# An LSTM in a two-layer kernel: the sums of four gates in two PSUM tiles instead of four, two sets of them, and their seeds in wider products spread over three steps

## The chip, the cores and the metric

The kernel runs on one core of a Trainium2 chip. The metric is the device time in microseconds of one execution, as the median of repeated runs; all times below are microseconds unless they are marked otherwise. The engines are PE (TensorE, with its weight loads listed as PEld), DVE (VectorE), ACT (ScalarE), POOL (GpSimd) and SP (SyncE, which issues DMAs).

## What is computed

The reference is a model of two layers on x of shape (8, 512, 256). Each layer has four parts: a conditioning step, an attention, a second conditioning step that is a recurrence over the 512 time steps, and a feed-forward part. In the first layer the recurrence is an LSTM with 256 hidden values and a batch of 8, and it is the only part that the change touches:

```python
xW = jnp.einsum('ntd,dg->ntg', x, Wx) + b
def step(carry, xw_t):
    prev_h, prev_c = carry
    a = xw_t + prev_h @ Wh
    i = jax.nn.sigmoid(a[:, :Hdim])
    f = jax.nn.sigmoid(a[:, Hdim:2 * Hdim])
    o = jax.nn.sigmoid(a[:, 2 * Hdim:3 * Hdim])
    g = jnp.tanh(a[:, 3 * Hdim:])
    next_c = f * prev_c + i * g
    next_h = o * jnp.tanh(next_c)
    return ((next_h, next_c), next_h)
```

Each step needs the h of the step before, so the 512 steps form one chain. All data are float32.

## The kernel before

The kernel runs its stages one after the other: the first layer's attention with its edge sums, the LSTM (function `lstm`, line 592), the routed heads, the second layer's attention, and a second recurrence with a mixture of experts. Inside the LSTM the orders of PE, ACT and DVE are written out by hand (`manual_schedule`): each of these engines runs its instructions in the order in which the program's text issues them. The framework adds the semaphores that data and memory need; it doesn't reorder these three engines.

**One step.** The 1024 gate values of a batch row are spread over four groups of 32 partitions (j = 0 to 3), 64 columns for each gate in each group. Each of the four gates, in the order f, i, g, o, has a PSUM tile of its own of 128 x 64 (`pgf`, `pgi`, `pgg`, `pgo`, made on line 618's list `banks`, with the column at which the gate lies in a weight row of 256). Line 678 multiplies the last h (kept in `ring`) with `wh`: two halves of the contraction (k) times four groups (j) make 8 matmuls for a gate, which are 16 matmul and 16 weight-load instructions on PE. Four time steps share a tile: step `now` of a group of four uses rows 8 * now to 8 * now + 7 of each 32. Its products cover the rows before them too, which nobody reads any more. The products are added to what already lies in the tile.

Then DVE transposes each gate's tile in 32 x 32 blocks into `G` (line 684), in the order f, i, g, o, and after each, ACT takes the sigmoid or tanh (line 685). After g's transpose DVE multiplies the old cell with f (line 687), after o's it runs a scan that gives the new cell (line 692). ACT takes the tanh of the cell (`th`, line 694), DVE multiplies it with o and writes the new h into `ring` (line 695), and PE can start the next step.

**The seeds.** What the products are added to is x's projection for four time steps, `xw`, brought into the tile's rows by a product with a selection matrix `pick` (function `seed`, line 648; its matmuls are line 652). In the last step of each group of four, after the four gates' transposes, 16 matmuls (4 gates x 4 groups of partitions, 64 columns each) seed all four tiles for the next four steps. They are 32 matmul and 32 weight-load instructions.

**The pieces.** Work of other stages is cut into pieces that are issued behind the ring write of chosen steps: gating pieces (`rest`, lines 534 to 552: eight for each 16 steps, the first two with PE work, the others ACT and DVE work), pieces of adaptive weights (`extra`, lines 1079 to 1089: PE products, DVE adds, and SP's DMAs of the next `w`, `b` and of the result `wd`), and the projection of the next 16 time steps (`project`, lines 637 to 645: two POOL copies, then eight PE products of 256 columns, with four DVE adds). In a step without PE work in a piece, a product whose result nobody reads (`fill`, line 708) keeps PE occupied; a step that seeds counts as having PE work. Every eighth step also sums `ring` on DVE (`hpart`, line 711) and copies it on ACT (`hT`, line 712).

Of the kernel before, what the change touches and what calls it, by code (L numbers as in the profile page):

```python
# [10 lines left out]
F32 = mybir.dt.float32  # L11
# [8 lines left out]
P = 128  # L20
B = 8
S = 512
# [352 lines left out]
class Edges:  # L375


    G = 8
# [213 lines left out]
def lstm(K, hT, rest, weights, extra, pp):  # L592

    nc, inp = K.nc, K.inp
    ident, xT = K.ident, K.xT
    mm = nc.tensor.matmul
    TT = nc.vector.tensor_tensor
    XB = GT
    RB = 8
    with ExitStack() as es:
        wp = K.pool(es, "l_w")
        sp = K.pool(es, "l_s", 3)  # L610
        xp = K.pool(es, "l_xw", 2)
        psx = K.pool(es, "l_px", 1, PSUM)
        extra = extra(K.pool(es, "l_pa", 1, PSUM))
        psg = K.pool(es, "l_pg", 1, PSUM)
        wx, wh, bias = weights
        pick = wp.tile([P, XB, B], F32, name="pick")
        nc.vector.tensor_copy(pick, ident.rearrange("p (b t) -> p t b", b=B))
        rings = [wp.tile([P, 2, 1 + RB, B], F32, name=f"ring{i}") for i in range(2)]
        for t in rings:
            nc.vector.memset(t[:, :, 0], 0.0)  # L620
        banks = [(psg.tile([P, 64], F32, name=f"pg{n}"), at) for n, at in (("f", 64), ("i", 0), ("g", 128), ("o", 192))]
        NC = 2 * B
        lefts = [wp.tile([P, 2 * NC], F32, name=f"left{i}") for i in range(3)]
        rights = [wp.tile([P, 2 * NC], F32, name=f"right{i}") for i in range(3)]
        cells = [wp.tile([P, 2 * NC], F32, name=f"cell{i}") for i in range(3)]
        for t in (*lefts, *cells):
            nc.vector.memset(t, 0.0)

        def half(w, n):
            return w.rearrange("p (k b two) -> p two k b", k=2, two=2)[:, n]  # L630

        def project(t0, pools=(psx,)):

            xw = xp.tile([P, 1024], F32, name="xw", tag="xw")
            xc = xp.tile([P, 2, P], F32, name="xc", tag="xc")
            for k in range(2):
                nc.gpsimd.tensor_copy(xc[:, k].rearrange("p (b t) -> p b t", b=B), xT[:, k, :, t0 : t0 + XB])  # L637
            yield xw
            for n in range(4):
                c = slice(n * 256, n * 256 + 256)  # L640
                px = pools[n % len(pools)].tile([P, S], F32, name="px", tag=("px", "pv")[n % len(pools)])[:, 0:256]
                for k in range(2):
                    mm(px, xc[:, k], wx[:, k, c], start=(k == 0), stop=(k == 1))  # L643
                    if k == 1:
                        nc.vector.tensor_tensor(xw[:, c], px, bias[:, c], ALU.add)
                    yield True

        def seed(t, xw):
            for dst, at in banks:
                for j in range(4):  # L650
                    c = j * 256 + at
                    mm(dst[32 * j : 32 * j + 32], pick[:, t % XB : t % XB + 4].rearrange("p t b -> p (t b)"), xw[:, c : c + 64], start=True, stop=True)

        proj = project(0, (psx, pp))
        xw = next(proj)
        for _ in proj:
            pass
        proj = iter(())
        nxt = None
        seed(0, xw)  # L660
        for _ in range(3):
            next(rest)
        E = mybir.EngineType
        K.marks = []
        es.enter_context(K.tc.manual_schedule(engines={E.PE, E.Activation, E.DVE}))
        for t in range(S):
            ring, at, now = rings[t // RB % 2], t % RB, t % 4
            for dst, c in banks:
                for k in range(2):
                    if t == 0:  # L670
                        hp = K.h0T[:, k, :]
                    elif at == 0:
                        hp = rings[1 - t // RB % 2][:, k, RB]
                    else:
                        hp = ring[:, k, at - now : at + 1].rearrange("p t b -> p (t b)")
                    for j in range(4):
                        w = wh[:, k, j * 256 + c : j * 256 + c + 64]
                        mm(dst[32 * j : 32 * j + B * (now + 1)], hp, w, start=False, stop=(k == 1), skip_group_check=True)  # L678
            left, right, cell, was = lefts[t % 3], rights[t % 3], cells[t % 3], cells[(t - 1) % 3]
            sf = sp.tile([P, 2, B], F32, name="sf", tag="sf")  # L680
            so = sp.tile([P, 2, B], F32, name="so", tag="so", bufs=2)
            for n, (to, f) in enumerate(((sf, AF.Sigmoid), (half(right, 0), AF.Sigmoid), (half(left, 1), AF.Tanh), (so, AF.Sigmoid))):
                G = sp.tile([P, 2, 32], F32, name="G", tag=f"G{n}")
                nc.vector.transpose(G.rearrange("p k b -> p (k b)"), banks[n][0])  # L684
                nc.scalar.activation(to, G[:, :, B * now : B * now + B], f)  # L685
                if n == 2:
                    TT(half(right, 1), sf, half(was, 1), ALU.mult)
            if now == 3 and t + 1 < S:
                if (t + 1) % XB == 0:
                    xw = nxt  # L690
                seed(t + 1, xw)
            nc.vector.tensor_tensor_scan(cell, left, right, 0.0, ALU.mult, ALU.add)
            th = sp.tile([P, 2, B], F32, name="th", tag="th")
            nc.scalar.activation(th, half(cell, 1), AF.Tanh)  # L694
            K.marks.append(TT(ring[:, :, at + 1], so, th, ALU.mult))  # L695
            at = t % XB
            busy = now == 3
            if at in (8, 13, 15, 0, 1, 2, 3, 4):
                busy |= next(rest, None) is True
            if at in (1, 2, 7, 11):  # L700
                busy |= next(extra, None) is True
            if at == 4 and t - 4 + XB < S:
                proj = project(t - 4 + XB)
                nxt = next(proj)
            elif at in (5, 6, 8, 9, 10, 12, 13, 14):
                busy |= next(proj, None) is True
            if not busy:
                mm(psx.tile([P, S], F32, name="fill", tag="px")[:, 0:256], ident, wx[:, 0, 0:256], start=True, stop=True)
            if t % RB == RB - 1:
                done = ring[:, :, 1:].rearrange("p k t b -> p k b t")  # L710
                nc.vector.tensor_reduce(K.hpart[:, t // RB % 16], done, AX.X, ALU.add)
                nc.scalar.copy(hT[:, :, :, t - RB + 1 : t + 1], done)
            if t % 64 == 5 and t > 64 or t == S - 3:
                n = t // 64
                n -= t < S - 3
                part = K.hpart[:, n % 2 * 8 : n % 2 * 8 + 7 + (n < 7)]
                nc.vector.tensor_reduce(K.hpart[:, 16 + n], part.rearrange("p n k b -> p k b n"), AX.X, ALU.add)
        for _ in extra:
            pass
# [685 lines left out]
XB = 16  # L1405
# [712 lines left out]
```

## Time and profile before

| what | us |
|---|---|
| median of 11 runs | 3889.5 (3885.09 to 3893.92) |
| the profiled execution, its device time | 3888.33 |
| its span, first to last instruction | 3886.6 |
| LSTM: start of the first ring write (L695) | 452.50 |
| LSTM: start of the last ring write | 1613.13 |
| the window 449 to 1614: PE busy, DVE busy, ACT busy | 939.68, 816.00, 611.89 |
| granted TensorE clock in that window, share of full speed | 1.00 |
| PE matmul and weight-load instructions in that window | 37845 and 37843 |

A row of the timeline gives the start from the span's begin, the duration, the engine, the line of the kernel, the operation, output and inputs, and how many instructions were merged (x16); in square brackets, how long the engine had been idle before and who released it. "issue" as releaser means that the engine waited for nothing that the profile shows. PE's matmuls overlap each other, so the durations of merged rows of two gates overlap too. A row of waits gives the time in total, the number of waits, and the longest.

### The profile page before, as it was taken

The numbers are of one execution on the slowest core, as the hardware profiler recorded it, in microseconds if no ns is written. First come the engines' busy times: TensorE is split into PE (matmuls) and PEld (weight loads), VectorE is DVE, ScalarE is ACT, GpSimd is POOL, SyncE is SP. The second block draws the span as 40 slices with busy tenths as digits, with TensorE's granted clock in tenths as the row PEclk, the third lists the DMA queues.
The fourth block names the chain that finished last, engine by engine and source line by source line (L and its number), as shares of the span: only waits on it lengthen the run. The fifth ranks groups of instructions, "written<-read, shape, count | busy, mean of one in ns | idle before, by whom it ended". The sixth has DMA issues, their size and how long they took to land.

```text
span 3886.6 us, 146241 instructions
## 1 busy us (share of the span) xinstructions
PE 3460.2 (89%) x62442; PEld 2319.0 (60%) x62442; DVE 2374.0 (61%) x8871; ACT 1618.1 (42%) x5695; POOL 668.3 (17%) x1479
## 2 busy tenths in 40 slices
PE   8999888888888888799989999999999899999986
PEld 5533455555555655466556666666666666666665
DVE  4488667767777767567657667666767533243444
ACT  3111255555555555455534444444444322232334
POOL 1010000000000000000023223222323111234366
PEclk9999999999999999999999999999999999999999
DMA  3022000000000000200000000000000060122245
GB/s 111 29 82 71 30 21 21 17 22 16 5 5 4 5 4 16 77 18 26 3 2 1 1 1 2 1 2 2 1 7 1 5 207 18 59 70 84 84 126 163
DMA packets 102924, 137.91 MB, mean 35 GB/s; under 512 B 12336, under 2 KB 84048, under 8 KB 102144
## 3 DMA queue, kind: packets, MB, share of 16 engines
q1 hardware_dynamic: 88416, 89.03, 7.4%
q0 software_dynamic: 11040, 34.29, 2.7%
q8 instruction: 490, 8.03, 0.9%
q10 hardware_dynamic: 2816, 5.24, 0.4%
q14 instruction: 162, 1.33, 0.1%
HBM read 86.44 MB, written 43.25 MB: 33 GB/s over the span
## 4 chain that ended last, share of the span: by engine, by line
PE 66%; ACT 14%; DVE 12%; issue 5%; POOL 1%; DMA 1%; ACTq 0%; POOLq 0%; SPq 0%; DVEq 0%
PE pgf L678 5%; PE pe L1237 4%; PE pg L1505 4%; PE po L1295 3%; PE pt L1280 3%; DVE G L684 3%; PE pp L1197 3%; PE pg L1738 3%; PE U L489 3%; PE px L1316 3%; PE pk L468 3%; ACT th L694 3%; ACT so L685 2%; PE pg L1484 2%; ACT left L685 2%
## 5 line engine op out<-in xcount | busy, mean ns | idle before, releaser
L678 PE MATMUL pgf<-wh,ring 128*16 128x64 f32 x8176 | 215.9, 223 | 201.6 <-DVE ring L695 198.4
L1508 DVE STREAM_TRANSPOSE ring<-h 128x64 f32<-128x64 f32 x512 | 125.6, 245 | 397.1 <-ACT h L1507 377.9
L678 PEld LDWEIGHTS pgf<-wh,ring 128*16 128x16 f32 x8176 | 127.8, 99 | 393.6 <-DVE ring L695 392.6
L1257 ACT ACTIVATE sm<-sm,nm 128x388 f32<-128x388 f32 (+3 forms) x512 | 283.6, 555 | 182.1 <-DVE nm L1253 182.0
L685 ACT ACTIVATE sf<-G 128x16 f32<-128x16 f32 x512 | 110.5, 216 | 464.2 <-DVE G L684 464.2
L1507 ACT ACTIVATE h<-pg 128x64 f32<-128x64 f32 x512 | 114.8, 224 | 453.2 <-PE pg L1505 400.5
L1505 PE MATMUL pg<-down,ring 128*16 128x64 f32 x8176 | 240.7, 223 | 30.5 <-DVE ring L1508 23.8
L1282 ACT COPY eT<-pt 128x512 f32<-128x512 f32 (+1 forms) x192 | 105.6, 550 | 357.4 <-PE pt L1280 357.2
L1197 PE MATMUL pp<-hn,wqkv 128*128 128x512 f32 x512 | 243.2, 619 | 0.8 <-DVE hn L1182 0.8
L1280 PE MATMUL pt<-ident,sm 128*128 128x128 f32 x1280 | 192.6, 283 | 56.8 <-DVE sm L1263 42.5
L1280 PEld LDWEIGHTS pt<-ident,sm 128*128 128x128 f32 x1280 | 148.1, 143 | 138.9 <-issue 81.9
L1264 POOL COPY pme<-sm 128x4 f32<-128x4 f32 x512 | 119.8, 235 | 646.5 <-DVE sm L1263 642.6
L678 PE MATMUL pgo<-wh,ring 128*16 128x64 f32 x8176 | 216.8, 220 | 14.2 <-issue 14.1
L678 PE MATMUL pgg<-wh,ring 128*16 128x64 f32 x8176 | 213.3, 220 | 4.8 <-issue 4.7
L684 DVE STREAM_TRANSPOSE G<-pgf 128x64 f32<-128x64 f32 x512 | 127.7, 249 | 138.7 <-PE pgf L678 132.7
L637 POOL COPY xc<-xT 128x128 f32<-128x128 f32 x64 | 17.1, 296 | 1136.0 <-DVE xT L552 1100.9
L678 PE MATMUL pgi<-wh,ring 128*16 128x64 f32 x8176 | 210.0, 220 | 1.2 <-issue 1.2
L1253 DVE CUSTOM_DVE_ANT_0 sm<-pe,mask 128x260 f32<-128x260 f32 (+2 forms) x384 | 141.7, 425 | 88.2 <-PE pe L1237 87.7
L1738 PE MATMUL pg<-xT,w 128*128 128x128 f32 x992 | 167.3, 295 | 17.8 <-POOL w L1718 12.7
L1263 DVE TENSOR_SCALAR sm<-sm,rc 128x388 f32<-128x388 f32 (+3 forms) x512 | 176.1, 387 | 9.0
L695 DVE TENSOR_TENSOR ring<-so,th 128x16 f32<-128x16 f32 x512 | 90.0, 176 | 147.3 <-ACT th L694 147.3
L643 PE MATMUL px<-wx,xc 128*128 128x256 f32 x512 | 174.4, 425 | 5.1 <-POOL xc L637 5.0
(513 smaller groups left out, 8284.5 us busy)
## 6 DMA issues: line engine op xcount, KB each, us to landing
cb<-order POOLq DMA_DIRECT2D x32, 512.0 KB
x<-xs SPq DMA_DIRECT2D x124, 128.0 KB
ys<-y SPq DMA_DIRECT2D x124, 128.0 KB
xs<-zero SPq DMA_DIRECT2D x66, 128.0 KB
w<-in_ada_w_dram SPq DMA_DIRECT2D x16, 512.0 KB
w<-in_moh_w_dram SPq DMA_DIRECT2D x32, 195.0 KB
xres<-xp SPq DMA_DIRECT2D x32, 128.0 KB
xc<-xres SPq DMA_DIRECT2D x32, 128.0 KB
```

Of the source, the lines that this page charges most:

```text
L643: mm(px, xc[:, k], wx[:, k, c], start=(k == 0), stop=(k == 1))
L678: mm(dst[32 * j : 32 * j + B * (now + 1)], hp, w, start=False, stop=(k == 1), skip_group_check=True)
L684: nc.vector.transpose(G.rearrange("p k b -> p (k b)"), banks[n][0])
L685: nc.scalar.activation(to, G[:, :, B * now : B * now + B], f)
L1197: mm(pp, T.wqkv[:, k, 0 : 2048].rearrange("p (i g h n) -> p i g h n", i=2, g=4, h=2)[:, i, g, h], self.hn[b][:, k, :], start=(k == 0), sto ...
L1237: mm(pe[a][:, 0 : w - lo], q[r, h, at], k[r, h, lo:w], start=(h == 0), stop=(h == 1))
L1253: nc.vector.tensor_tensor_reduce(out=sm[a][:, lo:w], in0=pe[a][:, 0 : w - lo], in1=T.mask[:, S - n + lo : 4 + S], scale=-1.0 / 8.0, scalar ...
L1257: nc.scalar.activation(sm[a][:, 0:w], sm[a][:, 0:w], AF.Exp, bias=nm[:, a : a + 1], scale=-1.0, accum_out=su[:, a : a + 1])
L1263: nc.vector.tensor_scalar(sm[a][:, 0:w], sm[a][:, 0:w], rc[:, a : a + 1], None, ALU.mult)
L1280: nc.tensor.transpose(pt[:, at, :], sm[i * m + a][:, 4 + j * P : 4 + (j + 1) * P], K.ident)
L1505: mm(pg[32 * j : 32 * j + B * (now + 1)], hp, M.wh[:, k, 64 * j : 64 * j + 64], start=False, stop=(k == 1), skip_group_check=True)
L1738: mm(pg, W[m][:, k * D + g * P : k * D + (g + 1) * P], X[m][:, k, :], start=(k == 0), stop=(k == 1))
```

## The change

The four tiles `pgf`, `pgi`, `pgg`, `pgo` are replaced by two tiles of 128 x 2 x 64, `pgig` (i in its first half, g in its second) and `pgfo` (f, then o), and there are two sets of these two tiles. A group of four time steps uses one set and the next group uses the other. A tile takes one PSUM bank, so the number of banks is four as before. The gates are still summed in the order f, i, g, o and transposed in the same order, each from its half.

A seed now brings in both gates of a tile with one product of 2 x 64 columns, for one group of partitions j: `seed(t, j, xw)` makes two matmuls of 128 columns. The seeds of the next group of four go into the other set, j = 0 and 1 in the first step of a group, j = 2 in the second and j = 3 in the third; the fourth has none. Eight matmuls replace sixteen. The projection that is being read (`xw = nxt`) is exchanged at step 12 of sixteen instead of step 15.

Of the pieces, the gating piece of step 8 of sixteen moves to step 14, and the projection's eight pieces, formerly in steps 5, 6, 8, 9, 10, 12, 13 and 14, are now in steps 5 to 12. A step that seeds no longer counts as one with PE work, so that each step without PE work in a piece gets a fill.

```diff
@@ -618,7 +618,8 @@
         rings = [wp.tile([P, 2, 1 + RB, B], F32, name=f"ring{i}") for i in range(2)]
         for t in rings:
             nc.vector.memset(t[:, :, 0], 0.0)
-        banks = [(psg.tile([P, 64], F32, name=f"pg{n}"), at) for n, at in (("f", 64), ("i", 0), ("g", 128), ("o", 192))]
+        banks = [[psg.tile([P, 2, 64], F32, name=f"pg{n}{i}") for n in ("ig", "fo")] for i in range(2)]
+        gates = [(1, 0, 64), (0, 0, 0), (0, 1, 128), (1, 1, 192)]
         NC = 2 * B
         lefts = [wp.tile([P, 2 * NC], F32, name=f"left{i}") for i in range(3)]
         rights = [wp.tile([P, 2 * NC], F32, name=f"right{i}") for i in range(3)]
@@ -645,11 +646,10 @@
                         nc.vector.tensor_tensor(xw[:, c], px, bias[:, c], ALU.add)
                     yield True
 
-        def seed(t, xw):
-            for dst, at in banks:
-                for j in range(4):
-                    c = j * 256 + at
-                    mm(dst[32 * j : 32 * j + 32], pick[:, t % XB : t % XB + 4].rearrange("p t b -> p (t b)"), xw[:, c : c + 64], start=True, stop=True)
+        def seed(t, j, xw):
+            x = xw[:, j * 256 : j * 256 + 256].rearrange("p (a g n) -> p g a n", a=2, g=2)
+            for g, dst in enumerate(banks[t // 4 % 2]):
+                mm(dst[32 * j : 32 * j + 32], pick[:, t % XB : t % XB + 4].rearrange("p t b -> p (t b)"), x[:, g], start=True, stop=True)
 
         proj = project(0, (psx, pp))
         xw = next(proj)
@@ -657,7 +657,8 @@
             pass
         proj = iter(())
         nxt = None
-        seed(0, xw)
+        for j in range(4):
+            seed(0, j, xw)
         for _ in range(3):
             next(rest)
         E = mybir.EngineType
@@ -665,7 +666,8 @@
         es.enter_context(K.tc.manual_schedule(engines={E.PE, E.Activation, E.DVE}))
         for t in range(S):
             ring, at, now = rings[t // RB % 2], t % RB, t % 4
-            for dst, c in banks:
+            for bank, a, c in gates:
+                dst = banks[t // 4 % 2][bank][:, a]
                 for k in range(2):
                     if t == 0:
                         hp = K.h0T[:, k, :]
@@ -681,28 +683,29 @@
             so = sp.tile([P, 2, B], F32, name="so", tag="so", bufs=2)
             for n, (to, f) in enumerate(((sf, AF.Sigmoid), (half(right, 0), AF.Sigmoid), (half(left, 1), AF.Tanh), (so, AF.Sigmoid))):
                 G = sp.tile([P, 2, 32], F32, name="G", tag=f"G{n}")
-                nc.vector.transpose(G.rearrange("p k b -> p (k b)"), banks[n][0])
+                nc.vector.transpose(G.rearrange("p k b -> p (k b)"), banks[t // 4 % 2][gates[n][0]][:, gates[n][1]])
                 nc.scalar.activation(to, G[:, :, B * now : B * now + B], f)
                 if n == 2:
                     TT(half(right, 1), sf, half(was, 1), ALU.mult)
-            if now == 3 and t + 1 < S:
-                if (t + 1) % XB == 0:
+            if now < 3 and t - now + 4 < S:
+                if t % XB == XB - 4:
                     xw = nxt
-                seed(t + 1, xw)
+                for j in ((0, 1), (2,), (3,))[now]:
+                    seed(t - now + 4, j, xw)
             nc.vector.tensor_tensor_scan(cell, left, right, 0.0, ALU.mult, ALU.add)
             th = sp.tile([P, 2, B], F32, name="th", tag="th")
             nc.scalar.activation(th, half(cell, 1), AF.Tanh)
             K.marks.append(TT(ring[:, :, at + 1], so, th, ALU.mult))
             at = t % XB
-            busy = now == 3
-            if at in (8, 13, 15, 0, 1, 2, 3, 4):
+            busy = False
+            if at in (13, 14, 15, 0, 1, 2, 3, 4):
                 busy |= next(rest, None) is True
             if at in (1, 2, 7, 11):
                 busy |= next(extra, None) is True
             if at == 4 and t - 4 + XB < S:
                 proj = project(t - 4 + XB)
                 nxt = next(proj)
-            elif at in (5, 6, 8, 9, 10, 12, 13, 14):
+            elif 4 < at < 13:
                 busy |= next(proj, None) is True
             if not busy:
                 mm(psx.tile([P, S], F32, name="fill", tag="px")[:, 0:256], ident, wx[:, 0, 0:256], start=True, stop=True)
```

## The prediction

> **What bounds the kernel now.** I read the page first, for the span and the costliest groups; then the timeline of a few recurrence steps, for the order inside one; then the starts of all 512 ring writes (L695), for how even the steps are; then PE's waits; and last one place of another stage that behaves as the new code will. The program has one long serial stage, the LSTM: the first ring write starts at 452.50 us, the last at 1613.13, so 1160.6 us hold 511 steps, 30% of the span. Inside it one step after the other looks like this:
>
> ```profile
> 1505.23 0.18 DVE L695 TENSOR_TENSOR ring<-so,th 128x16 f32<-128x16 f32 x1 [0.28 <-ACT th L694]
> ...
> 1505.46 0.42 PE L678 MATMUL pgf<-wh,ring 128*16 128x64 f32 x16 [0.49 <-DVE ring L695]
> ...
> 1505.92 0.41 PE L678 MATMUL pgg<-wh,ring 128*16 128x64 f32 x16
> 1505.94 0.25 DVE L684 STREAM_TRANSPOSE G<-pgf 128x64 f32<-128x64 f32 x1 [0.20 <-PE pgf L678]
> ...
> 1506.14 0.41 PE L678 MATMUL pgo<-wh,ring 128*16 128x64 f32 x16
> ...
> 1506.39 0.25 DVE L684 STREAM_TRANSPOSE G<-pgg 128x64 f32<-128x64 f32 x1
> ...
> 1506.67 0.22 ACT L685 ACTIVATE left<-G 128x16 f32<-128x16 f32 x1
> ...
> 1506.92 0.23 DVE L692 TENSOR_TENSOR_SCAN cell<-left,right 128x32 f32<-128x32 f32 x1
> ...
> 1507.18 0.22 ACT L694 ACTIVATE th<-cell 128x16 f32<-128x16 f32 x1
> ...
> 1507.43 0.18 DVE L695 TENSOR_TENSOR ring<-so,th 128x16 f32<-128x16 f32 x1 [0.28 <-ACT th L694]
> ```
>
> Columns are start, duration, engine, line, output and inputs. See the overlap: f's products end at 1505.88 (1505.46 + 0.42), and f's transpose starts 0.06 later, while PE still sums g and has o ahead of it. PE delivers a gate every 0.22 us and DVE turns each as it comes. So the period is a chain: 0.87 from PE's start to g's last product (1506.33), 0.06 to g's transpose, 0.28 to its tanh, 0.25 to the scan, 0.26 to th, 0.25 to the ring write, and 0.23 from there to PE's next start (1505.23 to 1505.46): 2.20. o is not in this chain. Its sums end at 1506.55 and its sigmoid at 1507.18, just as th begins. Of 511 steps, 446 take 2.19 to 2.24; I take 2.21. The rest of the 1160.6, 31 us above 511 x 2.21, sits in some sixty long steps, mostly the first of a group of four, and PE's waits show what they are:
>
> ```profile
> PE pgf L678 <- DVE ring L695: 198.4, 442, 1.6
> PE pgo L678 <- issue: 14.1, 22, 2.1
> PE pgg L678 <- issue: 4.7, 10, 0.8
> ```
>
> In these (us, times, longest) PE waits for nothing but its own instructions; all such waits of the stage add up to 21.9 us. The instruction queue moves 296 packets, 4.85 MB, during the stage.
>
> **The seeds today.** Every fourth step PE runs 64 more instructions (32 products, 32 weight loads; L652) after o's sums, 0.88 us in all, up to 1502.84 in the group that starts at 1501.96. The next step's PE start is 1503.26, 0.23 after its ring write, as in every other step. So the seeds cost nothing on the chain; they only lengthen the burst before the steps that stall for instructions.
>
> **The change, part by part.**
>
> (1) *f and o in one bank, i and g in another.* All four gates' sums are issued first, f, i, g, o, and then the transposes f, i, g, o (DVE keeps that order). If a read of one half of a bank has to wait for every earlier write to that bank, f's transpose waits for o's last product, the last of the step, and i's for g's. Is that so? L684 never shows it, as each gate has a bank to itself. The nearest row is another stage's tile po (L923, L925): sixteen products fill its first half, sixteen the second, and only then ACT reads the first half.
>
> ```profile
> 1935.29 2.71 PE L923 MATMUL po<-eT,v 128*64 128x128 f32 x32
> ...
> 1938.05 0.81 ACT L925 ACTIVATE oT<-po,bg,gh 128x128 f32<-128x128 f32 x2 [2.02 <-PE po L923]
> ```
>
> ACT sat idle 2.02 us. Fourteen of the first sixteen products had started by 1936.6, at 0.39 to 0.48 each, so the first half was whole by about 1937.2; ACT began at 1938.05, 0.05 after the last of the thirty-two. The read waited for the half that it doesn't touch. I take the same for f.
>
> The rule that speaks against the change is on the Trainium skill's page "PSUM — Partial Sum Buffer", in the section on bank collisions: two engines must not touch one bank in the same 32 partitions at once, even at different columns, so they have to be ordered by bank and not by address. By this rule f's transpose waits, and the stage gets longer as summed below; by the row that f's transpose starts 0.06 after f's own products, taken over unchanged, the period would stay 2.21. No run here shows a collision.
>
> Price: f's transpose moves from 0.48 after PE's start to o's end, 1.09 (1506.55 - 1505.46), plus 0.04 to 0.06 (0.06 for f at 1505.94; 0.04 for o in a step where PE stalled, 535.68 to 535.72). I take 1.14. What is late next: everything behind it on DVE's queue, i, g, the product L687, o, the scan; ACT's four functions wait for them, PE for the ring. But with all sums ready the transposes no longer wait for one another's sums. Steps that follow a hpart reduction (L711) show this in part, since f's transpose starts late there:
>
> ```profile
> 1503.84 0.24 DVE L684 STREAM_TRANSPOSE G<-pgf 128x64 f32<-128x64 f32 x1
> 1504.00 0.21 DVE L684 STREAM_TRANSPOSE G<-pgi 128x64 f32<-128x64 f32 x1
> ...
> 1504.19 0.25 DVE L684 STREAM_TRANSPOSE G<-pgg 128x64 f32<-128x64 f32 x1
> ...
> 1505.23 0.18 DVE L695 TENSOR_TENSOR ring<-so,th 128x16 f32<-128x16 f32 x1 [0.28 <-ACT th L694]
> ```
>
> From f's transpose to the ring write: 1.39 here, 1.49 in the normal step. g's still waited for its sum (0.93 after PE's start at 1503.26); at the 0.16 of f to i it would come 0.03 earlier, so 1.36 is the lower end and 1.40 (the slowest of such steps) the upper. I take 1.37, nearer the undisturbed case. New period: 1.14 + 1.37 + 0.23 = 2.74, with ends 1.13 + 1.36 + 0.23 = 2.72 and 1.16 + 1.40 + 0.23 = 2.79. Against 2.21: 0.53 a step, 512 x 0.53 = **+271 us** (261 to 297).
>
> (2) *Seeds of two gates in one product, over three steps.* 16 products for 32, each twice as wide (128 columns). The gate sums give the price: 16 instructions over four column groups in 0.22, so each group does four in 0.22, 55 ns for 64 columns, 110 for 128 as an estimate. One j is four instructions, 0.44; the first step's two j take 0.44 side by side or 0.88 in turn. Nothing is read back for four steps, since the other set of banks is filled: no wait on DVE. Cover: PE's end at 1.09, plus 0.88, plus a fill or a px piece of 0.70 is 2.67, inside 2.74; cost nothing. Had the period stayed 2.21, the same sum would be late by 0.02 to 0.46 in every fourth step (3 to 59 us). That is what the cover is worth.
>
> (3) *Pieces placed anew, and fills in each fourth step.* The gating pieces move from step 8 to 14 of sixteen, the projection pieces to 5 to 12. Their DVE work (0.42 to 0.49) and ACT work (0.40 to 0.61) lie between the ring write and f's transpose, a gap that grows from 0.72 to 1.37 us: nothing. SP's DMAs (w, b, wd in the extra pieces) and POOL's two copies keep their steps. The projection for a block now ends at step 12 of sixteen; j = 3 reads its last quarter in step 14. No wait there.
>
> (4) *The instruction waits.* PE issues 148 instructions a step now ((37845 + 37843) / 512), 65 per us. The change takes off about 8 a step and stretches the step: 140 in 2.74 us is 51 per us, and the burst of each fourth step is spread. The 31 us can lose anything from nothing to all; no row shows this rate, so I take the middle, **-16**.
>
> Sum on the profiled execution (3888.33 us, span 3886.6; median of the runs 3889.5, so nothing to correct): 3888 + 271 - 16 = 4143, rounded to **4145 us**.
>
> **Rivals.**
>
> *Halves are independent (6%).* f's transpose starts 0.06 after its own sums as now. Speaks for it: nothing but today's L684 rows, where banks are separate; against: po. The chain stays 2.21, the instruction waits lose about 16 to 20 us, and if the two j run side by side the seeds add 3: about **3873 us**, faster. It decides at f's transpose: under 0.6 us after PE's start, this one holds; at 1.1 mine does.
>
> *The order is the other way round (4%)*: g's products wait for i's transpose in the same bank. i's transpose ends 0.96 after PE's start (1506.17 + 0.25 - 1505.46); g then needs 0.42 as f does after a pause, and ends near 1.43 in place of 0.87. That is 0.56 a step, 287 us, less 16: **4159 us**, by another wait. Against it: in po nothing was read before the last write, and the sums are issued first. It decides at g's products: a pause of 0.5 before them on PE.
>
> *The wait comes and PE slows too (3%).* PE would be busy about 1.9 of 2.74 us. The stage's granted clock is 1.00; 36 us after it, between pauses of PE of 2.5 to 4.9 us, it is 0.81. At 0.81 the sums take 1.35 for 1.09: another 131 us, **4276**. Against it: gaps here stay below 1.3 us, as every step keeps a fill or a piece (2.74 - 1.09 - 0.43 for the shortest), and one of 2.10 us (L678, issue) changed no duration after it.
>
> **How the numbers follow.** My case has 87%. Its ends: 3888 + 261 - 31 = 4118 and 3888 + 297 = 4185, and 10 us more if the first seeds and a fill overrun in some steps; the range is 4115 to 4195, takes in the reversed order, and leaves out the other rivals (9%) and little else. Under 0.2% (8 us, about what the runs can tell from no change) is 1%, faster 5%, slower 94%.
>
> **What would show it.** In the profile after: ring writes 2.7 to 2.8 apart; f's transpose 1.1 after PE's start and waiting for the tile that holds f and o, the other three close behind at 0.16 to 0.19; the LSTM stage near 1405 us; the seeds on PE behind o's sums, waited for by nobody; PE's issue waits below 22. Everything after the stage should only be shifted. I am wrong if f's transpose still overlaps o's products.

## The result, and the profile after

The changed kernel takes 4112.7 us (median of 8 runs, 4107.65 to 4115.37), the kernel before on the same chip 3889.5 (31 runs). The ratio is 1.0572, with a 95% interval of 1.0563 to 1.0581: slower by 223 us. The forecast was 4145 with a range of 4115 to 4195, so its sign and mechanism hold and the median lies 2.3 us below the low end. What failed are two sizes in its sum; the section on the prediction names them.

The profiled execution took 4120.28 (span 4118.5), 7.6 more than the median and inside the range. I divide its span as the prediction divided that of before, by the ring writes (now L698):

| | before | after | difference |
|---|---|---|---|
| up to the first ring write | 452.50 | 456.19 | +3.7 |
| LSTM: 511 times the median step (2.21, 2.71) | 1129.3 | 1384.8 | +255.5 |
| LSTM: what is above that | 31.3 | 2.1 | -29.2 |
| behind the last ring write | 2273.5 | 2275.4 | +1.9 |
| sum: the span | 3886.6 | 4118.5 | +231.9 |

The median steps are rounded to 0.01 us here and below, which can move up to 2.6 us between the two LSTM rows.

One step in the timeline of after, to be held against the ten rows shown of before (weight loads left out):

```profile
1503.77 0.18 DVE L698 TENSOR_TENSOR ring<-so,th 128x16 f32<-128x16 f32 x1 [0.28 <-ACT th L697]
...
1504.00 0.43 PE L680 MATMUL pgfo<-wh,ring 128*32 128x64 f32 x16 [0.55 <-DVE ring L698]
...
1504.25 0.63 PE L680 MATMUL pgig<-wh,ring 128*32 128x64 f32 x32
...
1504.70 0.41 PE L680 MATMUL pgfo<-wh,ring 128*32 128x64 f32 x16
...
1505.17 0.25 DVE L686 STREAM_TRANSPOSE G<-pgfo 128x64 f32<-128x64 f32 x1 [1.22 <-PE pgfo L680]
1505.34 0.34 DVE L686 STREAM_TRANSPOSE G<-pgig 128x64 f32<-128x64 f32 x2
...
1505.80 0.24 DVE L686 STREAM_TRANSPOSE G<-pgfo 128x64 f32<-128x64 f32 x1
1505.98 0.22 DVE L695 TENSOR_TENSOR_SCAN cell<-left,right 128x32 f32<-128x32 f32 x1
...
1506.24 0.22 ACT L697 ACTIVATE th<-cell 128x16 f32<-128x16 f32 x1
1506.49 0.18 DVE L698 TENSOR_TENSOR ring<-so,th 128x16 f32<-128x16 f32 x1 [0.28 <-ACT th L697]
```

f's sums end at 1504.43. Its transpose starts at 1505.17, 0.06 after o's (1504.70 + 0.41): 1.17 after PE's start, where before it was 0.48. DVE has sat idle for 1.22, and the bracket names `pgfo`. i and g follow in 0.34 together. PE's sums themselves have not changed: 1.11 from the first to the last, as before (1.09). What has changed is that nothing is read while they run.

PE's waits in the stage (us, times, longest) show the other term:

```profile
PE pgfo L680 <- DVE ring L698: 346.5, 511, 1.3
...
PE pgfo L680 <- issue: 0.3, 1, 0.3
```

Before, 21.9 us of issue waits stood here, in 42 waits; one of 0.3 us is left. PE now waits for the ring write in every step.

### The profile page after: what moved, and what is told of

Its sections match the earlier page's. It is cut to its first block, busy times and chain, and to the rows that moved or that the text cites. A ratio compares the mean times of both kernels' runs of the same rounds, so it can differ in the third digit from the quotient of the medians.

```text
span 4118.5 us, 142417 instructions
## 1 busy us (share of the span) xinstructions
PE 3565.3 (87%) x60530; PEld 2393.1 (58%) x60530; DVE 2314.3 (56%) x8871; ACT 1483.8 (36%) x5695; POOL 661.3 (16%) x1479
## 4 chain that ended last, share of the span: by engine, by line
PE 68%; DVE 19%; ACT 6%; issue 4%; POOL 1%; DMA 1%; ACTq 0%; POOLq 0%; SPq 0%; DVEq 0%
PE pgfo L680 9%; DVE G L686 8%; PE pgig L680 6%; PE pe L1240 4%; PE pg L1508 4%; PE po L1298 3%; PE pt L1283 3%; PE pp L1200 3%; PE U L489 3%; PE pk L468 3%; PE px L1319 3%; PE pg L1741 3%; ACT so L687 3%; DVE ring L698 2%; PE pg L1487 2%
## 5 line engine op out<-in xcount | busy, mean ns | idle before, releaser
L680 PE MATMUL pgfo<-wh,ring 128*16 128x64 f32 x16352 | 423.1, 221 | 346.8 <-DVE ring L698 346.5
L680 PEld LDWEIGHTS pgfo<-wh,ring 128*16 128x16 f32 x16352 | 274.4, 99 | 549.3 <-DVE ring L698 548.6
L686 DVE STREAM_TRANSPOSE G<-pgfo 128x64 f32<-128x64 f32 x1024 | 252.3, 246 | 473.8 <-PE pgfo L680 473.8
L680 PE MATMUL pgig<-wh,ring 128*16 128x64 f32 x16352 | 321.9, 219 | 0.0
L680 PEld LDWEIGHTS pgig<-wh,ring 128*16 128x16 f32 x16352 | 261.0, 100 | 0.0
L1240 PE MATMUL pe<-kt,qt 32*128 32x132 f32 (+3 forms) x2048 | 178.9, 464 | 0.0
L1508 PEld LDWEIGHTS pg<-down,ring 128*16 128x16 f32 x8176 | 152.7, 99 | 41.9 <-DVE ring L1511 32.4
```

Of the source, the lines that this page charges most:

```text
L686: nc.vector.transpose(G.rearrange("p k b -> p (k b)"), banks[t // 4 % 2][gates[n][0]][:, gates[n][1]])
L1240: mm(pe[a][:, 0 : w - lo], q[r, h, at], k[r, h, lo:w], start=(h == 0), stop=(h == 1))
L1508: mm(pg[32 * j : 32 * j + B * (now + 1)], hp, M.wh[:, k, 64 * j : 64 * j + 64], start=False, stop=(k == 1), skip_group_check=True)
```

## Experiments

The chips differ: the kernel before takes 3885.9 us on that of the first four runs, 3844.9 on that of `e5` to `e7`, 3891.3 on that of `e8` to `e11`, and 3845.7 on that of `e12`. So each kernel stands beside the kernel before on its own chip. The last three columns are of the profiled executions: "LSTM" is the time from the first to the last ring write, "step" the median of its 511 steps, "excess" what they take above 511 times that rounded median.

| kernel | us | before | ratio (95%) | LSTM | step | excess |
|---|---|---|---|---|---|---|
| `e1_pairs_alone` | 4130.2 | 3885.9 | 1.0629 (1.0611 to 1.0647) | 1402.5 | 2.71 | 17.7 |
| `e2_if_go` | 3973.4 | 3885.9 | 1.0224 (1.0207 to 1.0241) | 1246.8 | 2.43 | 5.0 |
| `e3_turn_early` | 3923.2 | 3885.9 | 1.0097 (1.0080 to 1.0114) | 1197.8 | 2.34 | 2.1 |
| `e4_tile_two_banks` | 4148.9 | 3885.9 | 1.0674 (1.0654 to 1.0694) | 1425.8 | 2.71 | 40.9 |
| `e5_gate_bank_two_sets` | 3891.4 | 3844.9 | 1.0125 (1.0110 to 1.0141) | 1207.4 | 2.28 | 42.3 |
| `e6_burst` | 4079.3 | 3844.9 | 1.0616 (1.0600 to 1.0632) | 1393.9 | 2.71 | 9.0 |
| `e7_pieces_alone` | 3853.6 | 3844.9 | 1.0024 (1.0015 to 1.0033) | 1173.3 | 2.21 | 44.0 |
| `e8_before_plus16` | 3964.7 | 3891.3 | 1.0183 (1.0167 to 1.0198) | 1241.0 | 2.22 | 106.6 |
| `e9_after_plus64` | 4267.9 | 3891.3 | 1.0960 (1.0943 to 1.0976) | 1539.2 | 2.92 | 47.1 |
| `e10_fg_wide` | 3881.4 | 3891.3 | 0.9970 (0.9958 to 0.9982) | 1154.9 | 2.25 | 5.1 |
| `e11_fg_narrow` | 3885.9 | 3891.3 | 0.9986 (0.9977 to 0.9995) | 1161.8 | 2.26 | 7.0 |
| `e12_fo_early` | 3823.4 | 3845.7 | 0.9939 (0.9926 to 0.9953) | 1138.5 | 2.22 | 4.0 |

### Where the wait comes from

**Other pairs.** My theory: a transpose waits for every product that was issued before it into its tile. Then the pairs decide, and f with i, g with o must be cheaper. Edit to after:

```diff
-        ... for n in ("ig", "fo")] for i in range(2)]
-        gates = [(1, 0, 64), (0, 0, 0), (0, 1, 128), (1, 1, 192)]
+        ... for n in ("if", "go")] for i in range(2)]
+        gates = [(0, 1, 64), (0, 0, 0), (1, 0, 128), (1, 1, 192)]
```

> The changed kernel, but f shares a bank with i and g with o. If a read waits for every earlier write to its bank, f's transpose starts behind i's sums (about 0.70 us after PE's start), and g's behind o's (about 1.15); from g's transpose to the ring write it is 1.04 in the kernel before, perhaps 0.04 less, and 0.23 to PE's next start: a step of 2.38 to 2.42 where the changed kernel has 2.71, and 3935 to 3975 us in all. If the cost lies in something else of the change (products on half a tile, the wide seeds, the pieces, the fills), nothing moves: 4113 us and 2.71.

Measured: step 2.43, and the kernel is 87.5 us above its before where after is 223.2 above. f's transpose now waits for i's products, and g's for o's, each starting 0.06 to 0.07 after the end of the pair's sums:

```profile
1506.95 0.64 PE L680 MATMUL pgif<-wh,ring 128*16 128x64 f32 x32 [0.27 <-DVE ring L698]
...
1507.40 0.63 PE L680 MATMUL pggo<-wh,ring 128*16 128x64 f32 x32
1507.65 0.38 DVE L686 STREAM_TRANSPOSE G<-pgif 128x64 f32<-128x64 f32 x2 [0.43 <-PE pgif L680]
...
1508.10 0.25 DVE L686 STREAM_TRANSPOSE G<-pggo 128x64 f32<-128x64 f32 x1
```

**Other order, same tiles.** The tiles stay; DVE's reads are issued between PE's sums. Edit to after, in the loop over gates:

```diff
+            for m, (bank, a, c) in enumerate(gates):
...
+                for n in ((0,), (), (1, 2), ())[m]:
+                    turn(n)
```

> The changed kernel with its pairs of gates, but f's transpose is issued right behind f's sums, and those of i and g behind g's sums, ahead of o's. If the wait comes from the order in which sums and transposes of one bank are issued, f's transpose is back at 0.48 us after PE's start, i's comes at 0.93 and g's at about 1.06: a step of 2.30 to 2.34, and 3905 to 3930 us in all. If a bank with two gates is read only when both halves are whole, whatever the order of issue, it stays at 4113 us and 2.71.

Measured: step 2.34. The timeline of this kernel, weight loads left out:

```profile
1504.11 0.42 PE L685 MATMUL pgfo<-wh,ring 128*16 128x64 f32 x16
1504.34 0.63 PE L685 MATMUL pgig<-wh,ring 128*16 128x64 f32 x32
1504.59 0.25 DVE L672 STREAM_TRANSPOSE G<-pgfo 128x64 f32<-128x64 f32 x1 [0.21 <-PE pgfo L685]
1504.88 0.22 ACT L695 ACTIVATE sf<-G 128x16 f32<-128x16 f32 x1 [1.03 <-DVE G L672]
1504.90 0.42 PE L685 MATMUL pgfo<-wh,ring 128*16 128x64 f32 x16
1505.04 0.38 DVE L672 STREAM_TRANSPOSE G<-pgig 128x64 f32<-128x64 f32 x2 [0.20 <-PE pgig L685]
```

f's transpose is back at 0.48 after PE's start and runs while PE sums into the other tile. o's sums, issued behind it into the same tile, start at 1504.90, after the read's end at 1504.84. So the wait goes both ways, and the order in which sums and reads of one tile are issued decides who waits. Of the 0.50 lost, 0.37 return without a change of tiles. The other 0.13 are i's: its transpose stands behind g's sums, at 0.93 after PE's start in place of 0.71.

**Bank or tile?** The prediction said bank. Here before's four gates each have a bank of their own again, but in two tiles of two banks:

```diff
-        banks = [(psg.tile([P, 64], F32, name=f"pg{n}"), at) for n, at in ...]
+        tiles = [psg.tile([P, 2, 512], F32, name=f"pg{n}") for n in ("ig", "fo")]
+        banks = [(tiles[1][:, 0, 0:64], 64), (tiles[0][:, 0, 0:64], 0),
+                 (tiles[0][:, 1, 0:64], 128), (tiles[1][:, 1, 0:64], 192)]
```

> The kernel before (its seeds, its pieces), with f and o in one tile and i and g in another, but each tile two banks long and each gate in a bank of its own. If the wait goes by banks, nothing changes: 3889 us, give or take 8, and a step of 2.21. If it goes by tiles, f's transpose waits for o as in the changed kernel, and the seeds wait for o's transpose as well: a step of 2.71 or more, 4150 to 4250 us.

The timeline, weight loads left out:

```profile
1504.38 0.42 PE L679 MATMUL pgfo<-wh,ring 128*16 128x64 f32 x16
1504.61 0.63 PE L679 MATMUL pgig<-wh,ring 128*16 128x64 f32 x32
1505.06 0.41 PE L679 MATMUL pgfo<-wh,ring 128*16 128x64 f32 x16
...
1505.53 0.25 DVE L685 STREAM_TRANSPOSE G<-pgfo 128x64 f32<-128x64 f32 x1 [1.00 <-PE pgfo L679]
1505.70 0.34 DVE L685 STREAM_TRANSPOSE G<-pgig 128x64 f32<-128x64 f32 x2
```

f's transpose starts at 1.15, after o's last product, though o lies in another bank: the step is 2.71 as in after. The semaphores of this program go by tile. That is the framework's ordering, seen from its effect; whether two tiles in one bank would be ordered as well was not tried. The Trainium skill, page "PSUM — Partial Sum Buffer", section "PSUM bank collisions raise a hardware error", asks for a guard by bank and 32 partitions, and by that rule this kernel could have kept 2.21. The measurement decides: in this program a bank of one's own doesn't help inside a shared tile, a tile of one's own does.

### What the second set and the spread seeds are worth

The pairs alone, with one set of tiles, wide seeds in one burst, and before's places of pieces and fills; and the same with two sets. Edit to after for the latter, `e6_burst`:

```diff
-            if now < 3 and t - now + 4 < S:
+            if now == 3 and t + 1 < S:
...
-                for j in ((0, 1), (2,), (3,))[now]:
-                    seed(t - now + 4, j, xw)
+                for j in range(4):
+                    seed(t + 1, j, xw)
...
-            busy = False
+            busy = now == 3
```

with the lists of steps for the pieces as in before. For the former, `e1_pairs_alone`, one line more:

```diff
-        banks = [[psg.tile(...) ... for n in ("ig", "fo")] for i in range(2)]
+        banks = [[psg.tile(...) ... for n in ("ig", "fo")]] * 2
```

> One part of the change alone: the two tiles for four gates, but one set of them, all seeds (wide ones) in the last step of four, the pieces and fills as before. A step of 2.71 as in the changed kernel; and since the seeds now have to wait for o's transpose (it ends about 2.04 us after PE's start) and need about 1 us, each fourth step ends 0.35 to 0.5 late, 45 to 64 us in all: 4150 to 4195 us. If the second set of tiles buys nothing, as the seeds were hidden in the kernel before, it is 4113 to 4125 us.

> The changed kernel with its pairs and two sets, but the eight wide seeds all in the last step of four, and the pieces and fills of the kernel before. A step of 2.71. If slack on PE is what ends the instruction waits, they stay near 2 us: 4110 to 4118 us. If the burst makes them, some come back: 4118 to 4140. As PE has no pause of 1 us behind o's sums here, none of the steps of 3.5 us and more that the kernel with one set shows.

Measured: 244 us above before with one set, 234 with two and a burst, 223 in after. In all three the median step is 2.71; the pairing is the whole loss, and the rest of the change gives some 20 us of it back. I had the seeds of one set 0.35 to 0.5 late. They are not: PE waits 80.6 us for the transposes, starts the seeds 1.74 after its own start, and ends them at 2.75, just as the next step may begin: that step's sums start 0.23 after the ring write, as in before.

Part of what `e1`, `e4` and `e6` have above the median is something else, a fall of the TensorE clock. The timeline of `e6_burst`, PE's rows and the ring writes:

```profile
504.74 0.41 PE L680 MATMUL pgfo<-wh,ring 128*8 128x64 f32 x16 [1.14 <-DVE ring L698]
...
505.41 0.40 PE L680 MATMUL pgfo<-wh,ring 128*8 128x64 f32 x14
...
506.56 0.27 PE L680 MATMUL pgfo<-wh,ring 128*8 128x64 f32 x2 [0.75 <-issue]
506.77 0.99 PE L711 MATMUL fill<-wx,ident 128*128 128x256 f32 x2
508.19 0.18 DVE L698 TENSOR_TENSOR ring<-so,th 128x16 f32<-128x16 f32 x1 [0.28 <-ACT th L697]
508.42 0.63 PE L680 MATMUL pgfo<-wh,ring 128*16 128x64 f32 x16 [0.67 <-DVE ring L698]
508.82 1.08 PE L680 MATMUL pgig<-wh,ring 128*16 128x64 f32 x32
...
511.71 0.18 DVE L698 TENSOR_TENSOR ring<-so,th 128x16 f32<-128x16 f32 x1 [0.28 <-ACT th L697]
```

The same stretch by windows (start and end, length, busy time of PE, PEld, DVE, ACT and POOL with their instructions, granted clock, DMA share, GB/s):

```profile
506.00:507.00 1.00, 0.43 (x3) 0.32 (x3) 0.12 (x1) 0.00 (x0) 0.00 (x0) 1.00 0.00 0
507.00:508.00 1.00, 0.76 (x2) 0.06 (x1) 0.89 (x6) 0.65 (x5) 0.00 (x0) 0.52 0.06 16
508.00:509.00 1.00, 0.58 (x24) 0.58 (x28) 0.58 (x3) 0.16 (x2) 0.27 (x2) 0.50 0.00 0
```

At 507 the clock falls to one half, all sums take 1.5 to 1.7 times as long, and the step is 3.52. PE had paused 1.14 ahead of the row at 504.74 and 0.75 ahead of that at 506.56, with 1.1 us of sums in between. `e4` shows the same in the first step of a group (clock 0.50 from 1500.55 to 1503.96). Of the steps that lie more than 0.75 above the median (34 in `e4`, 13 in `e1`, 7 in `e6`, none in after), the clock falls in 31, 8 and 4. All steps with a fall hold about 31 of the 41 us of `e4`, 8 of the 18 of `e1` and 3 of the 9 of `e6`, where I had expected none; more than half of the rest are waits for instructions. The seeding step of these three kernels has no fill. The Trainium skill, page "TensorE: Matmul & The Clock Gate", Part 1, gives half speed after an idle window of about 3.4 us; here no pause in the 3.4 us before the fall was longer than 1.14, so by this trace a window need not be quite idle: in the 3.41 us before each of the 42 falls in these three kernels, PE was busy for 1.26 to 1.79. That the fill in each fourth step is what keeps after at 1.00 is what these rows suggest; no run took only the fills away, and `e5` and `e9`, which have that fill, show one fall each.

### The pieces

Before, with only the gating and projection pieces at their new places:

```diff
-            if at in (8, 13, 15, 0, 1, 2, 3, 4):
+            if at in (13, 14, 15, 0, 1, 2, 3, 4):
...
-            elif at in (5, 6, 8, 9, 10, 12, 13, 14):
+            elif 4 < at < 13:
```

> The kernel before with the pieces placed anew, its tiles, its seeds and its rule for fills as they were. If the placement is nothing, 3889 us, give or take 6. If it has a share in the instruction waits that went, down to 3860.

Measured +8.7 us. Two of sixteen steps (8 and 12) take 2.33, because projection pieces now follow the seed bursts of steps 7 and 11. In a step of 2.21 the new places cost; in one of 2.71 with spread seeds the same pieces cost nothing that the ring writes show.

### The instruction waits

The prediction left open how the 31 us depend on the rate. Two kernels raise it and leave the rest: 16 more PE instructions a step in before, and 64 in after, all into a spare tile that nobody reads (this work is added to the computation). Edit to before, behind each step's sums (after gets the same four times over):

```diff
+            for j in range(4):
+                mm(spare[32 * j : 32 * j + B], K.h0T[:, 0, :], wh[:, 0, j * 256 : j * 256 + 64], ...)
```

> The kernel before with four more products a step (16 instructions, into a bank that nobody reads, behind o's sums): 164 instructions a step. PE has room for their 0.06 us ahead of the next step. If the supply of instructions ends near 65 per us, the step becomes 2.52 on the mean: 100 to 125 us more (ratio 1.026 to 1.033). If the waits come from single bursts, a few us (ratio under 1.005).

> The changed kernel with sixteen more products a step (64 instructions, 0.22 to 0.44 us, behind o's sums, into a bank that nobody reads): 204 instructions in 2.71 us, 75 per us. If the supply ends near 65 per us, the step becomes about 3.1 on the mean, 200 us more than the changed kernel (4310). If slack on PE is what ends the waits, whatever the rate, it stays within 20 us of 4113.

Measured: +73 us over before, +153 over after (each against the kernel before on its own chip). Both kernels come to rest at the same rate. The stretch 470 to 1600 by windows, of `e8`:

```profile
470.00:1600.00 1130.00, 919.28 (x38253) 679.50 (x38246) 748.20 (x3739) 554.05 (x2506) 15.49 (x58) 0.99 0.04 11
```

and of `e9`:

```profile
470.00:1600.00 1130.00, 973.28 (x38288) 734.75 (x38277) 565.18 (x3006) 348.90 (x2009) 12.18 (x46) 1.00 0.04 11
```

Matmuls and weight loads together are 76499 and 76565 in 1130 us: 67.7 and 67.8 per us. No run here gave PE more in this stage. I had assumed 65, before's rate, hence too large expectations. With 67.8 the sizes come out: 164 instructions of a step in `e8` need 2.42 (mean step 2.43), 204 in `e9` need 3.01 (mean 3.01). That is the same count read the other way; what it adds is that two kernels that ask for different amounts settle at one rate. PE's waits in `e8`:

```profile
PE pgf L679 <- DVE ring L698: 138.5, 391, 1.5
PE pgo L679 <- issue: 35.8, 57, 2.4
PE pgi L679 <- issue: 15.7, 29, 1.9
PE pgx L681 <- issue: 15.7, 27, 1.1
PE pgg L679 <- issue: 13.9, 25, 1.0
```

Such waits now come in all four steps of a group (61, 58, 22 and 25 of them), where in before 29 of 42 were in the first.

The DMA records show what PE waits for. Its instructions arrive as packets of 16 KB on a queue of their own, q8. In 470 to 1600 this row (packets, MB, share of 16 engines' span) is the same in `e8` and `e9`:

```profile
q8 instruction: 299, 4.90, 1.9%
```

That is one packet for 256 of PE's instructions, every 3.78 us; before has 288 in this stretch, after 229. In before, `e8` and `e9` together 183 issue waits are longer than 0.5 us, and every one of them ends 1.2 to 1.6 us after such a packet has landed. So what PE lacks in these waits is the next packet. In `e9` PE is also nearly full (busy 973 of 1130 us), but in `e8` it still waits 138.5 us for the ring write, so the common rate isn't PE's own speed.

**Spread or rate?** A gate's own tile and both sets in it, narrow seeds spread over steps, new pieces: the burst goes, the number of instructions stays. ACT zeroes each half ahead of its seed, which is added work:

```diff
+                    nc.scalar.activation(banks[n][:, (t // 4 + 1) % 2], ident[:, 0:64], AF.Copy, scale=0.0)
...
+            if now and t - now + 4 < S:
...
+                for n in ((0,), (1,), (2, 3))[now - 1]:
+                    seed(t - now + 4, n, xw)
```

> A try at a version that beats both: a tile for each gate as before, but two sets of 64 columns in it, so that no transpose waits for another gate and the seeds can still be spread: f's in the second step of a group, i's in the third, g's and o's in the fourth, behind the pieces. They stay narrow, 16 products. As two sets share a tile, a set is first zeroed by ACT (0.2 us behind th, one to two in three of four steps) and the seeds are added to it. A step of 2.21. If the instruction waits of the kernel before come from the burst of seeds, they go as in the kernels with spread seeds (2 to 5 us of 31 left): 3858 to 3866 us. If they come from PE's rate of instructions, which is as before here, they stay: 3880 to 3895. If ACT's zeroing ends later than the ring write, up to 0.1 in three of four steps is lost: 40 us more.

Measured +46.5 us, an excess of 42.3 above the median step and issue waits of 14.9, 12.6 and 9.3 us for o, g and i. Spreading alone cures nothing. The kernel has a cost of its own besides: half of its steps take 2.28 to 2.29. In half of these, where ACT zeroes f's tile just ahead of f's sums, PE starts 0.32 after the ring write, not 0.23; what lengthens the others stays open.

Two kernels lower the number instead. f and g, neighbours in the weight row, share a tile; `e10` sums them with one product of 128 columns (112 instructions a step), `e11` with two of 64 (144), both with the seeds of f and g in one product:

```diff
-        banks = [(psg.tile([P, 64], F32, name=f"pg{n}"), at) for n, at in ...]
+        fg, i, o = [psg.tile([P, n], F32, name=f"pg{x}") for x, n in (("fg", 128), ("i", 64), ("o", 64))]
+        banks = [(fg, 64, 128), (i, 0, 64), (o, 192, 64)]
```

and in the loop over the sums, for `e11_fg_narrow` alone:

```diff
-            for dst, c, n in banks:
+            for dst, c, n in [(fg[:, 0:64], 64, 64), (fg[:, 64:128], 128, 64)] + banks[1:]:
```

> A pairing that should cost nothing: f and g share a tile and are summed in one product of 128 columns (columns 64 to 191 of a weight row), i and o keep tiles of their own, one set, the seeds in the last step and the pieces as in the kernel before. f's and g's transposes wait for the pair, whole at 0.64 us after PE's start, i's for 0.87; ACT takes f, g, i, and the scan can start when g's did before: a step of 2.21. PE issues 32 instructions a step fewer for the sums and 4 fewer for the seeds, about 112 a step. If its instruction waits come from the rate, 51 instructions per us for 65, the 31 us go: 0.8% faster than the kernel before (a ratio of 0.991 to 0.994). If they come from the burst of seeds alone, most of them stay (ratio 0.997 to 1.000). If the wider product or the new order costs something on the chain, the step is longer than 2.21.

> The same tiles and order, but f and g summed in products of 64 columns, each on its half: 144 instructions a step, a rate as in the kernel before. A step of 2.21 if the pair of f and g costs nothing; the instruction waits stay within some 10 us of those of the kernel before by the rate (ratio 0.996 to 1.001).

Both are slightly faster than before. `e10` has one issue wait of 1.4 us left, `e11` 2.9 us in five. The pair costs 0.04 to 0.05 a step, since f's transpose waits for g's sums (0.71 after PE's start), so little of the gain is left, and the ratio of `e10` falls where I had expected it if the waits stayed. Set side by side, by what a step asks for (instructions in 470 to 1600, carried to the mean step, over the median step), with the issue waits of the stage:

| kernel | instructions a step | asked per us | excess, us | issue waits, us |
|---|---|---|---|---|
| `e10` | 112 | 50 | 5.1 | 1.4 |
| after | 141 | 52 | 2.1 | 0.3 |
| `e2` | 141 | 58 | 5.0 | 2.2 |
| `e3` | 141 | 60 | 2.1 | 1.3 |
| `e11` | 144 | 64 | 7.0 | 2.9 |
| `e12` (below) | 143 | 65 | 4.0 | 1.6 |
| `e5` | 149 | 65 | 42.3 | 38.8 |
| before | 148 | 67 | 31.3 | 21.9 |
| `e7` | 148 | 67 | 44.0 | 24.4 |
| `e8` | 164 | 74 | 106.6 | 93.1 |

The waits rise steeply between 64 and 67 asked per us, just below the 67.8 that PE gets at most. Where in this stretch they begin stays open: `e12` and `e5` both ask for 65 and differ tenfold and more, but `e5`'s steps are uneven, and its short ones ask for 68 (149 in 2.20).

### A version that keeps both

f and o may share a tile and a seed product if f's transpose is issued right behind f's sums, ahead of o's; i and g keep tiles of their own. One set, before's pieces, 12 seed products in place of 16. Edit to before:

```diff
+        fo, i, g = [psg.tile([P, n, 64], F32, name=f"pg{x}") for x, n in (("fo", 2), ("i", 1), ("g", 1))]
+        banks = [(fo[:, 0], 64), (i[:, 0], 0), (g[:, 0], 128), (fo[:, 1], 192)]
...
+                if n == 0:
+                    nc.vector.transpose(G[0].rearrange("p k b -> p (k b)"), dst)
```

> The change's pair of f and o in one tile, with f's transpose issued right behind f's sums and so ahead of o's; i and g have tiles of their own; one set, seeds of f and o in one product, in the last step (behind those of i and g, as they wait for o's transpose), pieces as in the kernel before. o's sums start at 0.87 us after PE's start, f's transpose ends at about 0.75: the order costs nothing and the step is 2.21. PE is asked for 144 instructions a step, 65 per us, between the 64 at which few waits were seen and the 67 of the kernel before: a ratio of 0.993 to 0.998. If o's sums wait for f's transpose after all, the step is 2.25 and more and the ratio above 1.002.

```profile
1505.24 0.42 PE L680 MATMUL pgfo<-wh,ring 128*16 128x64 f32 x16
...
1505.69 0.41 PE L680 MATMUL pgg<-wh,ring 128*16 128x64 f32 x16
1505.72 0.25 DVE L682 STREAM_TRANSPOSE G<-pgfo 128x64 f32<-128x64 f32 x1 [0.34 <-PE pgfo L680]
...
1506.03 0.42 PE L680 MATMUL pgfo<-wh,ring 128*16 128x64 f32 x16
...
1507.21 0.17 DVE L699 TENSOR_TENSOR ring<-so,th 128x16 f32<-128x16 f32 x1 [0.28 <-ACT th L698]
```

o's sums wait for f's transpose and start 0.79 after PE's start (0.68 before), which costs next to nothing because o isn't in the chain: the step is 2.216, before's 2.208. The excess falls from 31.3 to 4.0, the issue waits from 21.9 to 1.6. Ratio 0.9939 (0.9926 to 0.9953), 22 us faster than before: the best version here.

## Why the prediction came out as it did

**(1) The wait: right, its reason half right.** f's transpose starts 0.06 after o's last product, at 1.17; the reversed order and independent halves are out by the first timeline, and `e2` and `e3` move the wait by moving pairs and order. But "if a read of one half of a bank has to wait" puts it down to the bank: by `e4` sharing a tile is enough, with a bank for each gate. Whether sharing a bank alone would do it too isn't known. On po, my evidence, both are the same thing.

**(1) The size of the step: 0.53 forecast, 0.50 measured, 15.5 us too much.** This is the term that put the range too high. The failing number is "1.36 is the lower end". From f's transpose to the ring write it takes 1.32. I had carried the 0.16 from f to i over to the gap from i to g; with both sums ready, that gap is 0.13, and the two transposes last 0.34 together (the median of all 1024 is 0.207 each; before's rows have 0.21 to 0.25). With 1.17 + 1.32 + 0.23 the step shown takes 2.72; the medians are 1.16, 1.32 and 0.23, in all 2.71. No row of before had three transposes with ready sums in a row (in its nearest rows g's still waited), so an end of 1.32 could have been reached only by allowing for a gap below the smallest one seen.

**(2) Seeds: right.** In after they end 2.16 after PE's start with the fill behind them, inside 2.71, and nobody waits for them.

**(3) Pieces: right for the step of 2.71.** At 2.21 they would have cost 9 us (`e7`).

**(4) The instruction waits: -16 forecast, -29.2 measured.** "I take the middle" failed. 52 per us is far below the onset at 64 to 67, so all of the waits had to go. The profile of before showed how steep this is, had I put the rate beside the waits: 67 asked per us, in a stage where PE stalls for instructions in only one step of twelve, is a supply that is only just missed.

**The rival of a slower PE** didn't occur in after (clock 1.00) but was no invention: it appears in `e1`, `e4` and `e6`, whose seeding step has no fill. The reading held against it, that a pause of 2.10 us "changed no duration after it", is wrong. The clock of before stood at 0.50 from 537.38 to 540.79, 2 us after that pause, and sums took 0.64 in place of 0.42:

```profile
535.40 0.28 PE L678 MATMUL pgo<-wh,ring 128*8 128x64 f32 x2 [2.10 <-issue]
...
536.64 0.42 PE L678 MATMUL pgf<-wh,ring 128*16 128x64 f32 x16 [0.34 <-DVE ring L695]
...
539.01 0.64 PE L678 MATMUL pgf<-wh,ring 128*24 128x64 f32 x16
```

There are three such falls in before's stage. The 0.81 behind the stage is also a mean: 13.65 of those 36 us stood at 0.50. In these rows a slower PE runs at half clock, not at 0.81.

**The sum.** On the profiled execution, 3888.33 + 255.5 - 29.2 + 3.7 + 1.9 = 4120.2, against 4143 forecast: 15.5 from the step, 13.2 from the waits, and 5.6 the other way outside the stage. The median lies 7.6 lower still. The low end allowed 3 us for that ("so nothing to correct") and set 261 against 255.5: with the step sized rightly, the median would have lain inside. What makes the profiled execution slower than the median isn't known: the others have no trace, their clock is 0.985 to its 0.983.

## What to carry over

When two results move into one tile, list for that tile the writes and reads in the order in which the program issues them: a read waits for every earlier write to the tile, a later write for the read, whichever halves or banks they touch. If a pair is wanted, issue the urgent read right behind its own sums and put the result that has slack second (`e12`). And work out the instructions per us of a stage of many small products: if it is within a few per cent of the supply, a few instructions less per step are worth more than spreading them.

## What the runs showed of the hardware

- PE was given at most 67.7 to 67.8 instructions per us over the stage (`e8`, `e9`), in packets of 256; its waits for them rose from 3 us at 64 asked (`e11`) to 22 at 67 (before), and the long ones ended 1.2 to 1.6 us after a packet had landed.
- The TensorE clock fell to 0.50 for some 7 us in `e6` after pauses of 1.14 and 0.75 with about 1 us of work between, and products took 1.5 to 1.7 times as long. In `e4` 31 falls of 3.41 us each came after 3.41 us in which PE was busy for 1.43 to 1.69.
- Of three 128x64 float32 transposes from PSUM in a row whose data are ready, the second starts 0.17 after the first (0.25 long) and the third 0.13 after the second (each 0.21 long; medians of after, `e4`, `e10` and `e11`). Whether two neighbours share a tile makes no difference: in `e10` the 0.17 lies inside a tile and the 0.13 between two, in after it is the other way.
